# Filler matmuls placed by TensorE's row activity, and other durations in a scheduling list

## The chip, the core and the metric

The kernel runs on one NeuronCore of a Trainium2 chip. The metric is the device time of one execution in microseconds (us), the median of three runs. One more execution was recorded by the hardware profiler; all durations below are from that one. The engines are TensorE (PE in the profile; PEld is its weight load), VectorE (DVE), ScalarE (ACT), GpSimd (POOL) and SyncE (SP), which here only issues DMAs.

## What is computed

Input x has shape (8, 256, 32, 32). Four layers follow each other, all in float32:

```python
# layer 0, per image: attention with 4 heads (q, k of 32 channels, v of 64), then a gated feed-forward
attn = softmax(einsum('bhkn,bhkm->bhnm', q, k) * SCALE)          # 1024 x 1024 for each head
out = einsum('bhdm,bhnm->bhdn', v, attn) + bn(dwconv3(v))
x = x + gamma1 * bn(conv1x1(out));  x = x + gamma2 * edffn(ln(x))
# layer 1: attention with 8 heads of 32 channels, then a small MLP
attn = softmax(einsum('bhdi,bhdj->bhij', q, k) * temp);  out = einsum('bhdj,bhij->bhdi', v, attn)
# layer 2: three quantized convolutions and a residual
# layer 3: a selective scan over 1024 positions, along rows and columns, forwards and backwards
dA = exp(dt[:, :, None] * A)                                      # A: 512 channels x 16 states
h = h * dA + dt[:, :, None] * B[:, None, :] * u[:, :, None]
y = einsum('bdn,bn->bd', h, C)
out = (y + x * D) * silu(z) @ W_out.T                             # the four directions are added
```

The first three layers work on one image at a time and are exact up to rounding; the fourth has 8 images x 4 directions.

## The kernel before, in words

**Two phases.** `phase_a` (from line 265) does layers 0 to 2 for the eight images and leaves layer 2's result in DRAM as bf16 codes. `phase_b` (from line 1142) does layer 3. Phase B starts when phase A has ended.

**The list.** Neither phase writes out its instruction order. Both are made of Python generators, called strands, that yield an operation (`_Op`), or a list of operations of one engine, or a condition to wait for. `_Order.run` (line 236) is a greedy list scheduler that runs while the program is built: for each ready strand it works out when its next operation could start (`start`, line 223), from when the engine becomes free, when the operands were written or last read, and 0.35 us between engines; it takes the earliest, then the strand's rank. `_Op.__init__` (line 103) gives each operation a planned duration, `cost`. The strand can override it: the maxima's matmuls yield 1.06, the scores' matmuls `SCORES`, and a list on TensorE gets `order.way` on top. `_Op.blocks` (line 129) cuts a tile into blocks of 512 elements; the list sees conflicts between operations by block. None of this exists on the chip: there, each engine runs its own instructions in the order that the list left, and waits at semaphores for real operands and buffers. So a planned duration changes only the order.

**Rooms.** `_Room` is a numbered set of equal buffers; `take` and `put` borrow and return one. In phase A the eight PSUM banks are one room (`bank`). In phase B the banks are four for `py`, three for `db` and one for `pp`.

**Phase A's two kinds of attention work.** `maxima` does a first pass for the softmax: two or four matmuls with 32 rows each (K = 32) fill two or four banks, then for each bank VectorE takes the maximum of each row (`tensor_reduce` into `stats`) and ScalarE the exponentials' sum (`activation` with `bias` and `accum_out`). `exponentials` then does the second pass: four score matmuls (K = 32), four that subtract the logarithm of the sum (`minus`, K = 3), four exponentials on ScalarE, four products with v. Strands of several images run side by side, held back by banks and ranks. Layer 0's feed-forward puts depthwise 3 x 3 taps on VectorE (`scalar_tensor_tensor`), ScalarE and GpSimd.

**Phase B's loop.** There are 64 blocks: 8 images x 2 orders of positions x 2 directions x 2 halves. Each block has 16 groups, one for each state. A group is four dbu = du x B on ScalarE (`scales`), 16 transposes into `db` (`turns`), four da = exp(dt x A) on ScalarE (`decays`, five buffers), four scans h on VectorE (`scans`), two products h x C on GpSimd (`products`) and 16 transposes into `py` that add up over the states (`sums`). Beside this, `ahead` starts the next blocks' work at fixed groups: the convolution `mixed` (xi with cvd into `pp`), the projection `dt` (xd with w_dt), and at group 6 `tables`: one list on ScalarE with a table load, Silu on xs, a table load, Softplus on dt, and the load of the exponential's table. The list marks dt as done at the end of that whole list. Then GpSimd forms tmp = dt x xs four times, TensorE transposes each into `pp`, and VectorE copies it to du, which the next block's dbu needs.

**Fillers.** `fill`, inside `phase_a` (line 1059), is called before each TensorE operation of phase A. If the planned gap, less 0.35 us, has room for at least one step of `FILL` = 0.3 us, it emits that many bf16 matmuls of `minus` (all -1) with itself, 128 rows x 512 columns, into a free bank, or into the operation's own bank. Their results are overwritten. The profile shows them as L1081. Phase B has none: its list has no `fill`.

## Time and profile before

| what | us |
|---|---|
| median of 3 runs (lowest to highest) | 10310.45 (10307.8 to 10314.3) |
| the profiled execution | 10303.42 |
| its span, first to last instruction | 10301.6 |
| busy in the span: PE, ACT, DVE, POOL | 9415.7, 8514.4, 7759.3, 6131.8 |

The profiled execution is 1.8 us longer than its span, and 7.0 us below the median. Phase A takes about the first 3690 us. `L136` in the profile is the line that emits every operation of the list, so groups are told apart by the names of their tiles. A float32 matmul of 512 columns stands in the trace as two MATMUL rows. "PEclk" is the share of TensorE's full clock that was granted. A busy engine in these views is one that has an instruction in flight; for TensorE that is not the same as an array in full use.

### The profile page before, as it was taken

The page shows a single profiled execution, that of the slowest core. Times are in us where ns is not written, and L with a number is a line of the kernel's source. Part 1 is how long each engine was busy: PE and PEld are TensorE (multiplying, and loading weights), DVE is VectorE, ACT ScalarE, POOL GpSimd, SP SyncE. Part 2 cuts the span into 40 slices and gives each one's busy share as a digit, 9 for nine tenths or more (in the row PEclk, how much of TensorE's full clock was granted, in tenths as well). Part 3 has the DMA queues.
Part 4 walks back from the last instruction along what each step waited for, and adds up shares of the span by engine and source line. Part 5 has one row for each costly group of instructions (what it writes and reads, how often), then busy time and mean ns, then how long its engine had stood idle before and what let it go on. Part 6 is the DMA issues. An engine that isn't in the chain of part 4 may idle for free.

```text
span 10301.6 us, 149772 instructions
## 1 busy us (share of the span) xinstructions
PE 9415.7 (91%) x55378; PEld 5953.1 (58%) x55499; DVE 7759.3 (75%) x8675; ACT 8514.4 (83%) x15869; POOL 6131.8 (60%) x2988
## 2 busy tenths in 40 slices
PE   9989989999999989989898999899989999989988
PEld 3333323333333347777776777777777777777676
DVE  6367467575667458888887888888888888888788
ACT  7867677867666759988898998989898889899888
POOL 1433032242121048878787787778787778787778
PEclk7988989989888899999999999999999999999999
DMA  2000000000000011112111112111111111111111
GB/s 58 30 19 17 21 21 19 17 26 17 13 17 9 17 34 51 53 44 59 46 52 53 46 52 59 43 52 56 49 51 48 56 50 49 55 52 46 57 43 52
DMA packets 219616, 415.83 MB, mean 40 GB/s; under 512 B 25137, under 2 KB 67505, under 8 KB 213762
## 3 DMA queue, kind: packets, MB, share of 16 engines
q1 hardware_dynamic: 218882, 406.24, 13.1%
q8 instruction: 437, 7.16, 0.3%
q14 instruction: 297, 2.43, 0.1%
HBM read 358.43 MB, written 37.22 MB: 38 GB/s over the span
## 4 chain that ended last, share of the span: by engine, by line
PE 28%; ACT 22%; DVE 8%; issue 3%; POOL 1%; DMA 1%; DVEq 0%; SPq 0%; POOLq 0%; ACTq 0%
PE pp L136 11%; PE py L136 9%; ACT da L136 9%; PE db L136 8%; ACT dbu L136 8%; DVE h L136 7%; ACT L136 2%; ACT xs L136 1%; ACT dt L136 1%; POOL h L136 1%; ACT L145 1%; DMA wi<-w_in 1%; DVE ys L136 1%; ACT st L136 0%; ACT z L136 0%
## 5 line engine op out<-in xcount | busy, mean ns | idle before, releaser
L136 POOL TENSOR_TENSOR h<-h,cb 128x1024 f32<-128x1024 f32 x2048 | 4813.3, 2373 | 1039.1 <-DVE h L136 367.0
L136 ACT ACTIVATE da<-dt,am 128x512 f32<-128x512 f32 x4096 | 2872.0, 714 | 543.2 <-DVE h L136 537.6
L136 ACT ACTIVATE dbu<-du,bT 128x512 f32<-128x512 f32 x4096 | 2798.1, 710 | 15.4 <-PE db L136 13.6
L136 PE MATMUL db<-ident,dbu 128*128 128x128 f32 x16384 | 2385.7, 280 | 362.2 <-DVE h L136 322.6
L136 DVE TENSOR_TENSOR_SCAN h<-da,db 128x512 f32<-128x512 f32 x2048 | 2338.9, 1202 | 460.2 <-ACT da L136 131.9
L136 DVE TENSOR_TENSOR_SCAN h<-da,st,db 128x512 f32<-128x512 f32 x2048 | 2465.9, 1262 | 258.8 <-ACT da L136 139.3
L136 PEld LDWEIGHTS db<-ident,dbu 128*128 128x128 f32 x16384 | 1885.2, 143 | 875.4 <-DVE h L136 539.6
L136 PE MATMUL py<-ident,h 128*128 128x128 f32 x16384 | 2141.8, 278 | 92.4 <-POOL h L136 75.5
L136 PEld LDWEIGHTS py<-ident,h 128*128 128x128 f32 x16384 | 1878.3, 143 | 227.0 <-POOL h L136 144.2
L136 DVE TENSOR_REDUCE stats<-bank 128x1 f32<-128x512 f32 x1536 | 983.4, 684 | 545.1 <-PE bank L136 544.0
L136 ACT ACTIVATE bank<-bank,stats 128x512 f32<-128x512 f32 x1536 | 1024.9, 672 | 432.1 <-DVE stats L136 424.5
L136 PE MATMUL bank<-big,big 32*128 32x512 f32 x4096 | 987.3, 713 | 37.9 <-ACT bank L136 27.7
L136 POOL TENSOR_TENSOR mid<-mid,mid 128x961 f32<-128x961 f32 (+2 forms) x192 | 397.2, 2076 | 992.9 <-ACT mid L136 663.6
L136 ACT ACTIVATE exps<-bank 128x512 f32<-128x512 f32 x1536 | 796.5, 620 | 165.9 <-PE bank L136 156.6
L136 PE MATMUL pp<-xi,cvd 128*128 128x512 f32 x1488 | 687.8, 598 | 1.6 <-DVE ys L136 1.6
L136 PEld LDWEIGHTS bank<-big,big 32*128 32x128 f32 x4096 | 334.7, 204 | 523.7 <-issue 219.7
L136 DVE SCALAR_TENSOR_TENSOR mid<-mid,cols,mid 128x961 f32<-128x961 f32 (+1 forms) x384 | 601.6, 1567 | 6.3
L136 PE MATMUL bank<-exps,big 128*32 128x512 f32 (+1 forms) x3072 | 547.9, 621 | 3.7 <-ACT exps L136 3.7
L136 PE MATMUL bank<-big 32*128 32x512 f32 x2048 | 517.4, 724 | 32.1 <-ACT bank L136 21.5
L136 POOL TENSOR_TENSOR tmp<-dt,xs 128x512 f32<-128x512 f32 x256 | 320.9, 1273 | 322.0 <-ACT dt L136 224.4
L136 POOL TENSOR_SCALAR big<-big,ga,gs 128x512 f32<-128x512 f32 x64 | 67.7, 1070 | 712.3 <-DVE gs L136 385.5
L136 POOL TENSOR_TENSOR big<-big,mid 128x961 f32<-128x961 f32 (+1 forms) x128 | 315.2, 2472 | 270.7 <-ACT mid L136 268.6
(204 smaller groups left out, 9116.4 us busy)
## 6 DMA issues: line engine op xcount, KB each, us to landing
cb<-c_d SPq DMA_DIRECT2D x1024, 256.0 KB, 3.3
wi<-w_in SPq DMA_DIRECT2D x192, 192.0 KB, 3.5
big<-in_x_dram SPq DMA_DIRECT2D x16, 1024.0 KB, 5.0
kept<-big SPq DMA_DIRECT2D x16, 1024.0 KB, 4.5
big<-kept SPq DMA_DIRECT2D x16, 1024.0 KB, 4.8
xf<-codes SPq DMA_DIRECT2D x48, 256.0 KB, 3.8
big<-big SPq DMA_DIRECT2D x16, 512.0 KB, 6.5
codes<-low SPq DMA_DIRECT2D x32, 256.0 KB, 2.0
```

Of the source, the lines that this page charges most:

```text
L136: return getattr(getattr(nc, self.engine), self.method)(*self.args, **self.kw)
L145: nc.scalar.preload_act_table_set("natural_log_exp_and_others")
```

## The change

It does four things.

- `fill` goes. `_Order.keep_dense` takes its place and is called for each TensorE operation in both phases. Each operation gets `rows`: its rows over 128, times its streaming time at full clock, half of that for transposes. The list keeps the planned activity of the last 3.4 us. Where that, with the operation itself, is under half of the window, or the planned gap is over 1.7 us, it emits fillers of 0.22 us into the buffer that came free first (or the operation's own fresh bank), as many as the gap holds, or up to 0.66 us past the time at which TensorE is free. Phase B gets a tile `minus` of its own and lends its `db` and `pp` banks.
- Planned durations change for all engines: among them, VectorE's three-operand operation between SBUF tiles of 961 elements from 1.07 to 1.45 us, ScalarE's maxima operation from 0.615 to 0.83 us, a decay or scale from 0.615 to 0.628 us; the maxima's matmuls from 1.06 to 0.9, `SCORES` from 1.3 to 1.12, `way` from 0.1 to 0.05.
- Blocks of small tiles become 64 elements instead of 512.
- A buffer that a DMA reads counts as read 2.1 us later.

```diff
@@ _Op.__init__
+        points = sum(math.prod(a.shape[1:]) == 1 for a in ins)
         if engine == "tensor":
...
+            self.rows = x.shape[0] / P * n * (0.44 if x.dtype != F32 else 1.72)
+            self.rows *= 0.5 if move else 1
         elif engine == "vector":
...
-            self.cost = 0.04 + n * (2.2 if scan else 0.57 if fast else 1.1) + (0.3 if fast or both else 0)
+            if method == "tensor_tensor_scan":
+                self.cost = 0.03 + 2.15 * n + 0.05 * points
+            elif both or three:
+                self.cost = 0.04 + 1.5 * n
+            elif fast:
+                self.cost = 0.04 + 0.9 * n
+            else:
+                self.cost = 0.05 + 1.09 * n + 0.05 * points
         elif engine == "scalar":
-            self.cost = 0.05 + 0.87 * n + (0.13 if len(ins) > 1 else 0)
+            self.cost = 0.05 + 0.06 * near + 0.85 * n + 0.093 * points + 0.17 * ("accum_out" in kw)
         elif engine == "gpsimd":
-            self.cost = 0.17 + 2.17 * n if method == "tensor_tensor" else 0.3 + n
+            self.cost = 0.12 + 2.2 * n if method == "tensor_tensor" else 0.07 + (2.0 if out.dtype == BF16 else 1.5) * n
@@ _Op.blocks
-        return [(a.name, k) for k in range(lo // 512, hi // 512 + 1)]
+        unit = 64 if step <= HALF else HALF
+        return [(a.name, k) for k in range(lo // unit, hi // unit + 1)]
@@ _Order
+    WINDOW, DENSE, DUMMY = 3.4, 0.5, 0.22
+
+    def keep_dense(self, t, cost, ops):
+        work = sum(o.rows for o in ops)
+        free, end = self.free.get("tensor", 0.0), t + cost
+        self.rows = [r for r in self.rows if r[1] > end - self.WINDOW]
+        seen = sum(w * (b - max(a, end - self.WINDOW)) / (b - a) for a, b, w in self.rows)
+        n = math.ceil((self.DENSE * self.WINDOW - seen - work * min(1.0, self.WINDOW / cost)) / self.DUMMY)
+        n = max(n, math.ceil((t - free - self.DENSE * self.WINDOW) / self.DUMMY))
+        if n > 0:
...
+            begin = max(free, since)
+            n = min(n, int((max(t, free + 0.66) - begin) / self.DUMMY))
+            if since < 1e9 and n > 0:
...
+                for _ in range(n):
+                    self.nc.tensor.matmul(x, lhsT=self.minus, rhs=rhs, start=True, stop=True)
...
+                t = max(t, begin + n * self.DUMMY)
+        self.rows.append((t, t + cost, work))
+        return t
@@ _Order.run
-            if self.fill and e == "tensor":
-                self.fill(t, ops)
+            if self.rooms and e == "tensor":
+                t = self.keep_dense(t, cost, ops)
             for o in ops:
                 o.emit(self.nc)
                 for k in o.reads:
-                    self.read.setdefault(k[0], {})[k] = (t + cost, e)
+                    self.read.setdefault(k[0], {})[k] = (t + cost + 0.7 * o.landing, e)
@@ phase_a
-    MAXIMA, SCORES = 2, 1.3
+    MAXIMA, SCORES = 2, 1.12
...
-                yield (1.06, ops)
+                yield (0.9, ops)
...
-    order.fill, order.way = fill, 0.1
+    order.rooms, order.minus, order.way = [bank], minus, 0.05
@@ phase_b
+    order.rooms = [ps_room, pp_room]
+    order.minus = wp.tile([P, P], BF16, name="minus", tag="minus")
+    nc.gpsimd.memset(order.minus, -1.0)
```

More of the change, by code (lines that the diff above doesn't have):

```diff
@@ L113, in __init__ @@
             n = math.prod(x.shape[1:]) / 1024
+            self.rows = x.shape[0] / P * n * (0.44 if x.dtype != F32 else 1.72)
             move = method == "transpose" or kw.get("is_transpose", False)
-            self.cost = max(0.06, (0.22 if x.shape[0] < 20 else 0) + n * (0.93 if move else 0.44 if x.dtype != F32 else 1.76 if n > 0.2 else 2.1))
+            self.cost = max(0.06, (0.22 if x.shape[0] < 20 else 0) + n * (0.96 if move else 0.44 if x.dtype != F32 else 1.76 if n > 0.2 else 2.0))
+            self.rows *= 0.5 if move else 1
         elif engine == "vector":
@@ L118, in __init__ @@
             both = near and method == "tensor_tensor"
-            scan = method == "tensor_tensor_scan"
-            self.cost = 0.04 + n * (2.2 if scan else 0.57 if fast else 1.1) + (0.3 if fast or both else 0)
+            three = near and method == "scalar_tensor_tensor"
+            if method == "tensor_tensor_scan":
[6 more added lines that the diff above has]
+                self.cost = 0.05 + 1.09 * n + 0.05 * points
         elif engine == "scalar":
-            self.cost = 0.05 + 0.87 * n + (0.13 if len(ins) > 1 else 0)
+            self.cost = 0.05 + 0.06 * near + 0.85 * n + 0.093 * points + 0.17 * ("accum_out" in kw)
         elif engine == "gpsimd":
-            self.cost = 0.17 + 2.17 * n if method == "tensor_tensor" else 0.3 + n
+            self.cost = 0.12 + 2.2 * n if method == "tensor_tensor" else 0.07 + (2.0 if out.dtype == BF16 else 1.5) * n
         else:
@@ L183, in __init__ @@
         self.free, self.written, self.read, self.base, self.last = {}, {}, {}, {}, {}
-        self.fill, self.way = None, 0.0
+        self.rooms, self.minus, self.way, self.rows, self.fresh = [], None, 0.0, [], {}
     def add(self, rank, strand):
@@ L213, in takes @@
             self.base[t.name] = self.last.get((room.tag, k), 0.0)
+            if room in self.rooms:
+                self.fresh[t.name] = t
             out.append(t)
@@ L234, in start @@
         return t
+    WINDOW, DENSE, DUMMY = 3.4, 0.5, 0.22
[7 more added lines that the diff above has]
+        if n > 0:
+            since, room, k = min(
+                ((self.last.get((r.tag, k), 0.0), j, k) for j, r in enumerate(self.rooms) for k in r.left),
+                default=(1e9, 0, 0),
+            )
+            x = self.fresh.get(ops[0].args[0].name)
+            if x is not None and self.base[x.name] < since:
+                since, room = self.base[x.name], None
+            begin = max(free, since)
+            n = min(n, int((max(t, free + 0.66) - begin) / self.DUMMY))
+            if since < 1e9 and n > 0:
+                if room is not None:
+                    room = self.rooms[room]
+                    room.left.remove(k)
+                    room.left.insert(0, k)
+                    x = room.take()
+                rhs = self.minus.unsqueeze(1).to_broadcast([P, 4, P])
+                for _ in range(n):
+                    self.nc.tensor.matmul(x, lhsT=self.minus, rhs=rhs, start=True, stop=True)
+                if room is not None:
+                    room.put(x)
+                    self.last[room.tag, k] = begin + n * self.DUMMY + self.LATENCY
+                self.rows.append((begin, begin + n * self.DUMMY, n * self.DUMMY))
+                t = max(t, begin + n * self.DUMMY)
+        self.rows.append((t, t + cost, work))
+        return t
     def run(self):
@@ L256, in run @@
                 for k in o.reads:
-                    self.read.setdefault(k[0], {})[k] = (t + cost, e)
+                    self.read.setdefault(k[0], {})[k] = (t + cost + 0.7 * o.landing, e)
                 for k in o.writes:
+                    self.fresh.pop(k[0], None)
                     self.written.setdefault(k[0], {})[k] = (t + cost + o.landing, e)
@@ L286, in phase_a @@
     OTHERS = 3
-    MAXIMA, SCORES = 2, 1.3
+    MAXIMA, SCORES = 2, 1.12
     GATE = 1
-    FILL = 0.3
     big = _Room(rooms, "big", NBIG, [P, CC, N])
@@ L1057, in emit @@
             nc.scalar.preload_act_table_set("natural_log_exp_and_others")
-    def fill(gap, ops):
-        free, o = order.free.get("tensor", 0.0), ops[0]
-        spare = min(bank.left, key=lambda k: order.last.get((bank.tag, k), 0.0), default=None)
-        own = o.method == "matmul" and o.kw["start"] and o.args[0].shape[-1] == HALF and o.kw["rhs"].shape[0] > 3
-        since = min(
-            [order.last.get((bank.tag, k), 0.0) for k in bank.left] + [order.base.get(o.args[0].name, 0.0)] * own,
-            default=1e9,
-        )
-        n = int((gap - max(free, since) - 0.35) / FILL)
-        if n < 1:
-            return
-        if spare is not None and order.last.get((bank.tag, spare), 0.0) <= since:
-            bank.left.remove(spare)
-            bank.left.insert(0, spare)
-            t = bank.take()
-        else:
-            t = None
-        out = o.args[0] if t is None else t
-        rhs = minus.unsqueeze(1).to_broadcast([P, 4, P])
-        for _ in range(n):
-            nc.tensor.matmul(out, lhsT=minus[:, : out.shape[0]], rhs=rhs, start=True, stop=True)
-        if t is not None:
-            bank.put(t)
-    order.fill, order.way = fill, 0.1
+    order.rooms, order.minus, order.way = [bank], minus, 0.05
     stage = [0] * B
```

## The prediction

> **What bounds the kernel now.** I read the page's slices first, then the windows table by stage, then windows on stretches at low clock, last the order in time inside them. The page gives TensorE's busy tenths and its granted clock:

> ```profile
> PE   9989989999999989989898999899989999989988
> ...
> PEclk7988989989888899999999999999999999999999
> ```

> By stage (us, then busy us and count of PE, PEld, DVE, ACT, POOL, then clock, DMA share, GB/s), phase A and the body of phase B:

> ```profile
> 0.00:3690.00 3690.00, 3460.72 (x14923) 1280.33 (x14923) 2220.47 (x3297) 2630.62 (x5719) 907.14 (x470) 0.89 0.06 21
> ...
> 3900.00:10180.00 6280.00, 5683.53 (x38842) 4478.63 (x38959) 5316.94 (x5161) 5655.86 (x9767) 5012.54 (x2396) 0.97 0.17 51
> ```

> Phase A: TensorE has work 94% of the time, ScalarE 71%, and the clock is 0.89. The trace grants 1 or 0.5, so 22% of phase A, about 812 us, is at half clock. Phase B: ScalarE is nearest its limit (90%), the clock is 0.97. Here are phase A's longest stretches at half clock and two short ones:

> ```profile
> 101.50:193.70 92.20, 91.66 (x217) 39.81 (x217) 66.74 (x104) 82.14 (x215) 27.90 (x13) 0.50 0.01 3
> 989.00:1036.80 47.80, 47.80 (x116) 19.04 (x115) 42.20 (x68) 37.03 (x107) 3.54 (x3) 0.50 0.00 1
> 2931.00:2968.00 37.00, 36.64 (x83) 11.25 (x81) 27.94 (x46) 21.71 (x60) 0.00 (x0) 0.50 0.00 0
> 3207.00:3272.00 65.00, 65.00 (x153) 24.66 (x153) 52.64 (x85) 42.59 (x118) 2.06 (x1) 0.51 0.00 0
> 3504.00:3535.00 31.00, 30.65 (x73) 9.59 (x72) 22.81 (x41) 16.57 (x47) 0.00 (x0) 0.51 0.00 1
> 2630.00:2654.00 24.00, 23.93 (x52) 8.49 (x52) 20.05 (x35) 17.59 (x50) 0.00 (x0) 0.52 0.00 0
> 572.00:586.00 14.00, 10.62 (x20) 5.14 (x20) 4.95 (x8) 13.97 (x31) 5.02 (x3) 0.52 0.00 0
> 555.00:569.00 14.00, 8.74 (x12) 3.16 (x12) 13.89 (x14) 8.97 (x18) 8.53 (x4) 0.52 0.00 0
> ```

> In the six long ones TensorE has an instruction in flight all the time and is still at half clock: "busy" is not what the clock follows. They are the maxima, whose matmuls use 32 rows, two at a time. Single rows of the order in time (start, us, engine, ...) give the prices: two matmuls of the maxima at full clock (four rows of the trace) and nine at half, one and two fillers, two of ScalarE's maxima operations:

> ```profile
> 1503.89 0.39 PE L1081 MATMUL bank<-minus 128*128 128x512 bf16 x1
> 1507.37 0.60 PE L1081 MATMUL bank<-minus 128*128 128x512 bf16 x2
> 2063.31 1.13 PE L136 MATMUL bank<-big 32*128 32x512 f32 x4
> 3219.14 7.35 PE L136 MATMUL bank<-big,big 32*128 32x512 f32 x18
> 3224.08 0.66 ACT L136 ACTIVATE bank<-bank,stats 128x512 f32<-128x512 f32 x1
> 3224.74 0.66 ACT L136 ACTIVATE bank<-bank,stats 128x512 f32<-128x512 f32 x1
> ```

> So a filler costs TensorE 0.60 - 0.39 = 0.21 us. A pair of the maxima takes 1.13 less the tail that a lone filler shows beyond its step (0.39 - 0.21), some 0.9 us, at full clock, and 7.35 x 4 / 18 = 1.63 at half. ScalarE needs 2 x 0.66 = 1.32 for it. Phase B loses its clock where ScalarE loads tables for Silu and Softplus; two such places:

> ```profile
> 5838.00:5840.00 2.00, 1.14 (x11) 0.91 (x10) 0.00 (x0) 1.98 (x5) 1.56 (x2) 1.00 0.00 0
> 5840.00:5842.00 2.00, 0.42 (x4) 0.18 (x2) 0.00 (x0) 1.99 (x5) 2.00 (x2) 1.00 0.00 0
> 5844.00:5846.00 2.00, 1.33 (x7) 0.96 (x6) 2.00 (x3) 2.00 (x6) 0.48 (x1) 0.50 0.07 27
> ...
> 5648.00:5654.00 6.00, 5.21 (x19) 3.05 (x18) 3.55 (x3) 4.42 (x8) 6.00 (x3) 0.52 0.19 65
> 5654.00:5660.00 6.00, 5.83 (x31) 3.13 (x30) 1.37 (x2) 2.37 (x6) 6.00 (x4) 0.91 0.20 53
> ```

> TensorE starves at 5838 to 5842, the clock halves, yet ScalarE stays full: nothing is lost there. In the second place ScalarE idles 5.2 us (6 - 4.42 + 6 - 2.37) after the half clock.

> **The change part by part.**

> *Fillers in phase A.* By the order of instructions they go from 955 to 1749, and from 347 to 1032 between matmuls of the maxima; elsewhere they are few more. 794 x 0.21 = 167 us of TensorE. Among long runs of pairs there stand one to five, some 2.4 a pair: 0.9 + 2.4 x 0.21 = 1.4 us, against 1.63 at half clock and ScalarE's 1.32. Row activity is then (0.45 + 0.5) / 1.4 = 0.68, well over 0.45, so the clock holds.

> *What the clock gives in phase A.* In each long stretch the next engine bounds the gain: 92.2 - 82.14, 47.8 - 42.2, 37 - 27.94, 65 - 52.64, 31 - 22.81, 24 - 20.05 = 49 us of 297 together, 17%; the pair's 1.4 for 1.63 says 14%. In the other 515 us at half clock ScalarE or VectorE is often full, as in the two short rows, so I take half that rate, 8%: 41 us. Together 90; the neighbours won't run at 100%, so two thirds: 60 us saved. Bounds: 0 and 90.

> *Fillers in phase B.* 1056, or 222 us of TensorE, nearly all at groups 7 to 10 of a block, ahead of the transposes of tmp: 16 a block, 3.5 us, against 2 + 2 - 1.14 - 0.42 = 2.4 us idle at 5838 to 5842 and more up to 5844. The table list counts dt as done too late, so the first transpose of tmp, at 5839.77, will come some 2 us later; du is wanted only in the next block, which hides it. Without that cover it is 2 us x 62 = 124 us.

> *What the clock gives in phase B.* Only where ScalarE idles after the gap. That is in two of eight blocks: 5.2 us above with a further 1.3 at 5660 to 5666, and about 2 us near 5450; 8.5 x 8 images = 68 us. Fillers stand there too, 28 to 30 a block. I take half: 30 us. Bounds: 0 and 68.

> *Fillers that do lie on the path.* The 109 of phase A outside the maxima, 23 us; I take 15, and 10 for waits for banks in phase B: 25 us lost.

> *The new durations.* They only reorder. VectorE's taps were planned at 1.07 us and now 1.45, against 1.57 in the trace: nearer. ScalarE's maxima operation goes from 0.615 to 0.83, against 0.66 from start to start: further off. Decays and scales go from 0.615 to 0.628; phase B's order on VectorE and GpSimd hardly changes, ScalarE's two streams interleave differently. No row prices a reordering; its size is bounded by ScalarE's idle time in phase B, 620 us, and by phase A's. I bound it at 100 us either way, by the half clock's own total gain, and take 0: one of the two large corrections helps, the other hurts. The DMA reading rule, smaller blocks and phase B's memset of one tile (0.2 us) go with this: 0.

> *Sum.* -60 - 30 + 25 = -65 us. The profiled execution at 10303.4 becomes 10238; the median stands 7.0 higher, so 10245.

> **Rivals.**

> 1. *The order gains too.* The taps' 384 operations no longer hold up the maxima behind them on VectorE. For it: ScalarE waits 424 us for `stats`. Against: the worse maxima duration. With 90 + 68 from the clock, no fill loss and some 30 from the order: 10310 - 188 = 10122.
> 2. *The clock is full and nothing follows.* The neighbours were the bound: gains 25, losses 25. For it: the short rows and 5844. Time 10310.
> 3. *Slower: the fillers make TensorE the bound of the maxima.* About two thirds of 768 pairs, 510, run at full clock now with 0.9 us under ScalarE's 1.32. The list plans ScalarE at 0.83, so 1.66 a pair, and fills for a gap that is 0.34 us narrower on the chip. A run of three to five makes the pair 1.5 to 1.95 us. At +0.3 us a pair, 153 us: 10245 + 153 = 10398. It decides from 65 / 510 = 0.13 us a pair. Against: the average of 2.4 gives 1.4, just at the point.
> 4. *It doesn't do what it says:* a stretch falls to half clock anyway, and its pair with fillers takes 1.63 + 2.4 x 0.43 = 2.7 us. Its row activity is then about 0.7, too little to return at once. 100 pairs would cost 107 us: 10350.

> **How the numbers follow.** Forecast 45%, rival 1 12%, rival 2 8%, rival 3 25%, rival 4 10%. A measurement here tells apart about 0.2%, 21 us. Faster 0.57, same 0.08, slower 0.35. Predicted 10245; its own range, from the bounds 0 to 90, 0 to 68 and the losses, is 10150 to 10290. The order's 100 us and rivals 1 and 3 widen it to 10080 to 10420.

> **What would show it.** Right: phase A's clock at 0.96 or more, no half-clock stretch over 15 us in the maxima, ScalarE busier in them; phase B at 0.99, with ScalarE's idle time after the gaps of two blocks in eight gone. Fillers hidden: no row of the waits in which ScalarE waits longer for `stats` than 424 us. Wrong: phase A is longer at a full clock (rival 3), the clock stays near 0.89 (rival 4), or phase B changes by more than 70 us, which would be the order's work.

## The result, and the profile after

| | before | after |
|---|---|---|
| median, us (lowest to highest, 4 runs each) | 10312.38 (10307.8 to 10321.5) | 10261.17 (10247.5 to 10281.83) |
| ratio, 95% interval | | 0.9952 [0.9939, 0.9964] |
| profiled execution, span | 10303.42, 10301.6 | 10256.65, 10254.8 |

The change saves 51 us, 0.5%; the forecast was 65. The sum came and its parts did not. The page's slices after:

```profile
PE   9999999999999989999999999999999999999998
...
PEclk9998999999999999999999999999999999999999
```

The windows by stage (us, then busy us and count of PE, PEld, DVE, ACT, POOL, then clock, DMA share, GB/s):

```profile
0.00:3690.00 3690.00, 3492.14 (x15717) 1243.67 (x15717) 2202.61 (x3291) 2635.16 (x5723) 921.63 (x474) 0.94 0.07 21
3900.00:10180.00 6280.00, 5832.44 (x40216) 4512.66 (x40214) 5357.52 (x5197) 5697.23 (x9827) 5051.02 (x2412) 1.00 0.18 52
```

Phase A's clock went from 0.89 to 0.94, yet ScalarE is busy only 4.5 us more in the same window (2635.16 for 2630.62). Phase B is at 1.00. Where the phases part is read from the tile view of `db`: its first transpose is the start of phase B's loop (count, then ns min/median/max, then first and last start).

```profile
L147 PE MATMUL db<-ident,dbu x16384: 270/273/477, 3769.7 to 10220.1; 128*128 128x128 f32 x200
```

The same row before:

```profile
L136 PE MATMUL db<-ident,dbu x16384: 272/273/477, 3763.5 to 10264.1; 128*128 128x128 f32 x200
```

So up to here the kernel is 6.2 us *later*, and the rest takes 6485.1 us (10254.8 - 3769.7) for 6538.1 (10301.6 - 3763.5): 53.0 us less. The costliest groups (busy us, mean ns | idle before, what ended it), four of before and then five of after:

```profile
L136 PE MATMUL db<-ident,dbu 128*128 128x128 f32 x16384 | 2385.7, 280 | 362.2 <-DVE h L136 322.6
L136 DVE TENSOR_REDUCE stats<-bank 128x1 f32<-128x512 f32 x1536 | 983.4, 684 | 545.1 <-PE bank L136 544.0
L136 ACT ACTIVATE bank<-bank,stats 128x512 f32<-128x512 f32 x1536 | 1024.9, 672 | 432.1 <-DVE stats L136 424.5
L136 PE MATMUL bank<-big,big 32*128 32x512 f32 x4096 | 987.3, 713 | 37.9 <-ACT bank L136 27.7
```

```profile
L147 ACT ACTIVATE da<-dt,am 128x512 f32<-128x512 f32 x4096 | 2863.9, 714 | 506.0 <-DVE h L147 502.0
L147 PE MATMUL db<-ident,dbu 128*128 128x128 f32 x16384 | 2329.7, 276 | 194.7 <-DVE h L147 157.7
...
L147 DVE TENSOR_REDUCE stats<-bank 128x1 f32<-128x512 f32 x1536 | 987.9, 684 | 655.0 <-PE bank L147 652.2
L147 ACT ACTIVATE bank<-bank,stats 128x512 f32<-128x512 f32 x1536 | 1024.7, 672 | 409.2 <-DVE stats L147 395.3
L147 PE MATMUL bank<-big,big 32*128 32x512 f32 x4096 | 928.3, 667 | 15.7 <-ACT bank L147 9.0
```

The maxima's matmuls are shorter (667 ns for 713), but VectorE waits longer for the banks they fill (652.2 us for 544.0): what their higher clock gave was lost again on TensorE. The page doesn't say to what; the experiments below do. In phase B the transposes' idle time fell from 362.2 to 194.7 us.

### The profile page after: what moved, and what is told of

Same layout as the page of the kernel before. It is cut to its first block, busy times and chain, and to the rows that moved or that the text cites. A ratio compares the mean times of both kernels' runs of the same rounds, so it can differ in the third digit from the quotient of the medians.

```text
span 10254.8 us, 153646 instructions
## 1 busy us (share of the span) xinstructions
PE 9573.8 (93%) x57349; PEld 5920.9 (58%) x57349; DVE 7741.9 (75%) x8671; ACT 8521.2 (83%) x15873; POOL 6150.3 (60%) x2993
## 4 chain that ended last, share of the span: by engine, by line
ACT 28%; PE 22%; DVE 10%; issue 2%; POOL 1%; DMA 1%; DVEq 0%; SPq 0%; POOLq 0%; ACTq 0%
ACT da L147 11%; ACT dbu L147 10%; PE pp L147 9%; DVE h L147 8%; PE py L147 7%; PE db L147 6%; ACT L147 2%; ACT xs L147 1%; ACT dt L147 1%; DMA wi<-w_in 1%; POOL h L147 1%; ACT L156 1%; DVE ys L147 1%; ACT st L147 1%; ACT z L147 0%
## 5 line engine op out<-in xcount | busy, mean ns | idle before, releaser
L147 ACT ACTIVATE da<-dt,am 128x512 f32<-128x512 f32 x4096 | 2863.9, 714 | 506.0 <-DVE h L147 502.0
L147 PE MATMUL db<-ident,dbu 128*128 128x128 f32 x16384 | 2329.7, 276 | 194.7 <-DVE h L147 157.7
L147 PEld LDWEIGHTS db<-ident,dbu 128*128 128x128 f32 x16384 | 1855.6, 141 | 798.8 <-DVE h L147 350.4
L147 PE MATMUL py<-ident,h 128*128 128x128 f32 x16384 | 2099.2, 274 | 95.4 <-POOL h L147 90.0
L147 PEld LDWEIGHTS py<-ident,h 128*128 128x128 f32 x16384 | 1837.4, 141 | 236.4 <-POOL h L147 179.2
L147 DVE TENSOR_REDUCE stats<-bank 128x1 f32<-128x512 f32 x1536 | 987.9, 684 | 655.0 <-PE bank L147 652.2
L147 ACT ACTIVATE bank<-bank,stats 128x512 f32<-128x512 f32 x1536 | 1024.7, 672 | 409.2 <-DVE stats L147 395.3
L147 PE MATMUL bank<-big,big 32*128 32x512 f32 x4096 | 928.3, 667 | 15.7 <-ACT bank L147 9.0
L277 PEld LDWEIGHTS <-minus 128*128 128x128 bf16 x2805 | 260.6, 101 | 663.4 <-issue 463.8
L277 PE MATMUL bank<-minus 128*128 128x512 bf16 x1749 | 508.5, 414 | 52.5 <-ACT bank L147 41.1
L147 PEld LDWEIGHTS bank<-big,big 32*128 32x128 f32 x4096 | 283.2, 191 | 463.0 <-issue 267.4
L147 POOL TENSOR_TENSOR big<-big,mid 128x992 f32<-128x992 f32 (+1 forms) x128 | 324.4, 2542 | 290.1 <-ACT mid L147 287.4
```

What stands on the lines that cost most here:

```text
L147: return getattr(getattr(nc, self.engine), self.method)(*self.args, **self.kw)
L277: self.nc.tensor.matmul(x, lhsT=self.minus, rhs=rhs, start=True, stop=True)
```

## The experiments

The question was why the clock pays in phase B and not in phase A. Three theories stood at the start. **O**: the new order loses what the clock gives. **N**: the neighbours (ScalarE, VectorE) were the bound of phase A, so the clock is worth nothing there. **F**: the fillers lie on TensorE's path and eat the gain. The table has every run; "to db" is where the first transpose into `db` begins, "rest" the span less that, "half" the time at half clock in either part, all from the profiled execution, "sent" the fillers of either phase. Each ratio is against executions of before taken together with that run; their medians lie between 10307.3 and 10312.4.

| run | sent A / B | half A / B | to db | rest | median, us | ratio to before, 95% |
|---|---|---|---|---|---|---|
| before | 955 / 0 | 850 / 387 | 3763.5 | 6538.1 | 10312.38 | |
| after | 1749 / 1056 | 437 / 41 | 3769.7 | 6485.1 | 10261.17 | 0.9952 [0.9939, 0.9964] |
| x1 | 1391 / 0 | 887 / 488 | 3869.3 | 6550.4 | 10420.64 | 1.0104 [1.0089, 1.0119] |
| x2 | 1250 / 899 | 625 / 219 | 3791.1 | 6549.3 | 10343.75 | 1.0024 [1.0010, 1.0037] |
| x3 | 0 / 0 | 1236 / 454 | 3804.7 | 6547.8 | 10350.09 | 1.0034 [1.0021, 1.0047] |
| x4 | 1343 / 1001 | 440 / 89 | 3670.6 | 6502.7 | 10191.27 | 0.9880 [0.9865, 0.9895] |
| y1 | 0 / 1056 | 1225 / 68 | 3775.1 | 6489.2 | 10262.41 | 0.9951 [0.9934, 0.9967] |
| y2 | 727 / 1056 | 884 / 55 | 3794.8 | 6488.6 | 10299.30 | 0.9991 [0.9984, 0.9998] |
| y3 | 1343 / 1056 | 447 / 55 | 3683.1 | 6491.8 | 10172.29 | 0.9862 [0.9847, 0.9876] |
| y4 | 1203 / 1056 | 597 / 48 | 3737.2 | 6488.3 | 10213.99 | 0.9906 [0.9891, 0.9921] |
| z1 | 1749 / 0 | 492 / 410 | 3783.1 | 6536.0 | 10313.09 | 1.0004 [0.9995, 1.0013] |
| z2 | 0 / 1056 | 1085 / 55 | 3729.5 | 6489.1 | 10214.20 | 0.9906 [0.9892, 0.9921] |
| z3 | 1343 / 1056 | 567 / 67 | 3778.9 | 6488.9 | 10272.15 | 0.9968 [0.9957, 0.9979] |
| z4 | 1748 / 1056 | 358 / 61 | 3685.6 | 6486.9 | 10164.30 | 0.9861 [0.9844, 0.9877] |

### One part of the change alone (x1, x2)

x1 is the kernel before with the new durations, blocks and read times and the old `fill`; x2 is the kernel after with the old durations, blocks and read times. Of x1's edit:

```diff
-            self.cost = 0.05 + 0.87 * n + (0.13 if len(ins) > 1 else 0)
+            self.cost = 0.05 + 0.06 * near + 0.85 * n + 0.093 * points + 0.17 * ("accum_out" in kw)
...
-    MAXIMA, SCORES = 2, 1.3
+    MAXIMA, SCORES = 2, 1.12
```

> The new durations, blocks and read times with the fillers of before: the old rule in phase A, none in phase B. Phase A is read up to the first transpose into db (before 3763.5 us, after 3769.7), phase B from there to the end (6538 and 6485). Phase A: if the new order loses what the clock gives (theory O), it is about 3800 us; if the neighbours are the bound (N) or the fillers lie on the path (F), about 3765. Phase B: if the fillers' clock is the gain, 6538; if the new durations are, 6485.

> The new fillers in both phases with the durations of before. Phase A: O says about 3725 us, N and F say about 3765. Phase B: 6485 if the clock is the gain, 6538 if the durations are. Clock 0.94 or more in phase A.

Both are slower than before, and the change that has both is faster: the parts don't add up. No theory had foreseen this: up to `db` it is 3869 us in x1, where 3800 was the highest figure expected, and 3791 in x2, where 3765 was; x2's rest is 6549 and not 6485 or 6538. Much of phase A's loss comes early. The 192nd of ScalarE's maxima operations, the last one before a long pause, ends at 335.5 us in x1 and 324.5 in x2, for 273.7 before: 62 of the 106 us that x1 loses up to `db`, and 51, more than the 28 that x2 loses there. Windows there, x1 first, then x2:

```profile
150.00:200.00 50.00, 50.00 (x102) 11.96 (x101) 22.74 (x36) 29.73 (x75) 11.33 (x5) 0.50 0.00 0
```

```profile
150.00:200.00 50.00, 50.00 (x102) 11.31 (x101) 22.10 (x35) 26.32 (x73) 2.64 (x2) 0.50 0.00 0
```

ScalarE is busy only 29.73 and 26.32 of 50 us, at half clock, with fillers among the matmuls.

### No fillers, and fewer (x3, x4)

x3 takes the fillers out of the kernel after, so that its list doesn't plan them either; x4 lowers the target and counts transposes whole.

```diff
-    order.rooms, order.minus, order.way = [bank], minus, 0.05
+    order.way = 0.05
-    order.rooms = [ps_room, pp_room]
```

> The changed kernel without any filler. Phase A's clock falls to 0.85 or less. N says that phase A stays within 20 us of 3770; if the clock is worth what the forecast says (14 to 17% of the long stretches), it is 3830 or more. Phase B: 6538 if the clock is the gain there, 6485 if the durations are.

```diff
-    WINDOW, DENSE, DUMMY = 3.4, 0.5, 0.22
+    WINDOW, DENSE, DUMMY = 3.4, 0.4, 0.22
...
-            self.rows *= 0.5 if move else 1
```

> The changed kernel with a target of 0.4 instead of 0.5 and transposes counted fully: 1343 fillers in phase A instead of 1749, 1001 in phase B instead of 1056. F says that phase A falls by 20 us or more, to 3750 or less, at nearly the same clock; N says 3765 to 3775. Phase B stays at 6485.

x3's 3804.7 lies between the two figures that its theories set, 3790 and 3830. The same 50 us in x3 and in after:

```profile
150.00:200.00 50.00, 49.17 (x131) 31.26 (x132) 40.62 (x77) 46.19 (x134) 6.48 (x3) 0.50 0.00 1
```

```profile
150.00:200.00 50.00, 50.00 (x191) 13.96 (x191) 37.33 (x64) 43.78 (x122) 7.57 (x4) 1.00 0.00 1
```

This is the pair of lines to remember. At half clock *without* fillers ScalarE does as much (46.19) as at full clock with them (43.78), and far more than at half clock with them (29.73, 26.32 above). x4 is 99 us shorter up to `db` than after at nearly the same time at half clock, as F had it; its rest missed the expected 6485 by 18 us. But x3 and x4 also have other orders of the real work than after, since the list plans around the fillers; they cannot tell F from O. The next runs hold the order still.

### The order held, the fillers not sent (y1, y2, z1)

The list plans its fillers as in after, so that every real instruction keeps its place, but phase A's are not sent (y1), or n // 2 of each group are (y2); in z1 phase A's are sent and phase B's are not. y1:

```diff
+                m = 0 if len(self.rooms) == 1 else n
                 if room is not None:
...
-                for _ in range(n):
+                for _ in range(m):
```

> The kernel after with its order of all real instructions in the first phase kept as it is (the planner still counts its 1749 fillers there), but none of those fillers is sent to TensorE; the second phase and its 1056 fillers are as after. Theory F (fillers lie on the path of the first phase: 1749 x 0.21 us = 373 us of TensorE time at full clock, part of it in front of real matmuls): without them the clock falls, but the path is relieved; the first phase is about 3770 again within 40 us, the clock of it about 0.85, median 10230 to 10300. Theory C (the clock is what these fillers buy, and they stand in gaps as planned): as the clock falls to half for about 1200 us, the first phase loses a fourth of that and more, 4000 or more, median over 10450. Theory T (only the long stretches at half clock with fillers in between cost much): the first maxima end at about 192 us as in the run without fillers.

> As the kernel after with its order kept, but of each group of n fillers in the first phase only n // 2 are sent (727 of 1749). F: fewer fillers on the path at a clock that still mostly holds: the first phase ends 40 to 100 us earlier than the 3770 of after, median 10160 to 10220. C: the clock falls and the time grows, 3830 or more, median over 10320. O (the gain of the run with a target of 0.4 came from another order of the real work, not from fewer fillers): with the order unchanged and the clock mostly held, 3770 within 20, median 10245 to 10280.

> The kernel after with its order of all real instructions kept in both phases; its 1749 fillers of the first phase are sent, of the 1056 of the second none (the planner still counts them). Theory C (the gain of the second phase is the clock that they hold): without them the second phase has 300 us and more at half clock again and takes 6530 to 6555, median 10300 to 10325. Theory O (the gain is the order that the planner makes when it has the new durations and fillers): 6485 within 15 although the clock falls, median 10250 to 10275. Theory P (both, the order with a clock that only TensorE's stretches need): between, 6500 to 6530.

First the 50 us of above once more, in y1, which has the order of after:

```profile
150.00:200.00 50.00, 49.17 (x130) 31.33 (x132) 40.54 (x77) 46.20 (x134) 6.40 (x3) 0.50 0.01 2
```

So the pair of lines does not come from another order. y1: 1749 fillers fewer, 788 us more at half clock, and the same time (10262.41 and 10261.17). In phase A the fillers are worth nothing in sum, as theory F of y1 had it, and not C, which asked for 4000 us up to `db`. T came too: y1's 192nd maxima operation ends at 278.6 us, as x3's does. What the clock gives and what the fillers cost is taken apart below. z1: without the 1056 of phase B, its rest takes 6536.0, and that of before is 6538.1: the gain of phase B is the clock that they hold (theory C), the order adds 2 us. (The eight runs with the second phase of after take 6485.1 to 6491.8 for it, so the gain is some 44 to 51 us.) z1's waits of the transposes and decays, as the page has them:

```profile
L147 ACT ACTIVATE da<-dt,am 128x512 f32<-128x512 f32 x4096 | 2867.8, 714 | 524.9 <-DVE h L147 519.6
L147 PE MATMUL db<-ident,dbu 128*128 128x128 f32 x16384 | 2399.6, 282 | 309.2 <-DVE h L147 282.0
```

After has 506.0 and 194.7 in these places. With equal orders one can follow the delay from instruction to instruction: both traces have 15643 ScalarE rows with the same names in the same order. Counted from 3800 us on, z1 falls behind after through all of phase B, by 9.4 us at 5000, 17.3 at 6000, 24.8 at 7000, 34.1 at 8000, 40.0 at 9000 and 50.8 at the end. But not every block adds to it. Phase B repeats every eight blocks, and cut at each block's first transpose into `db` the delay adds up over the eight repetitions to this:

```
block of eight       1     2     3     4     5     6     7     8
delay, us in sum   14.4   0.6   4.5  15.0  -0.1  -0.9  -0.1  17.7
```

So it stands in four blocks of eight, some 2 us each time in blocks 1, 4 and 8 and 0.6 in block 3. Half clock is not confined to these: of the 387 us at half clock in phase B of before (z1 has 410), 27.3, 54.6, 23.9 and 54.6 us lie in blocks 2, 5, 6 and 7, in each of which z1's delay is 0.6 us or less over the eight repetitions.

The same measure explains phase A. Here is how far y1 is behind after (negative: ahead), over after's stretches at half clock of more than 8 us:

```
stretch of after at half clock      fillers in it   y1 behind after, us
 957 to 1009                         41               10.4 -> -8.8
1282 to 1306                         18                2.2 -> -6.6
1719 to 1736                          7               -6.6 -> -15.1
2538 to 2551, 2620 to 2637           33               -0.2 -> -5.1, -0.9 -> -7.0
all 19 stretches, 300 us            184              -54.7 in sum
outside them                                         +60.1 in sum
```

Outside these stretches the fillers gain 60 us. In 300 us in which the clock falls all the same, they lose 55, of which the five shown make 47. y1 is at half clock for most of these five too (69 to 100% of each), so it is hardly the clock that sets the two apart there. A fallen stretch need not cost anything: that of 517 to 531 holds 17 fillers and loses nothing. VectorE is busy for 13.93 of its 14 us in after and in y1 alike, and TensorE has time to spare (9.85 us busy in y1). So N does not hold for phase A as a whole: the clock is worth something there, and what it gives is lost again elsewhere. The windows around the worst one, after and then y1, both at nearly the same low clock:

```profile
949.00:1009.00 60.00, 58.71 (x137) 14.36 (x141) 41.60 (x66) 32.76 (x92) 2.51 (x2) 0.57 0.00 0
```

```profile
949.00:1009.00 60.00, 58.69 (x134) 29.22 (x132) 57.44 (x92) 44.05 (x126) 5.48 (x4) 0.56 0.00 0
```

And TensorE's order in time there, in after (start us, us, ...):

```profile
959.44 1.03 PE L277 MATMUL bank<-minus 128*128 128x512 bf16 x2
960.40 2.08 PE L147 MATMUL bank<-big,big 32*128 32x512 f32 x4
962.41 1.03 PE L277 MATMUL bank<-minus 128*128 128x512 bf16 x2
963.37 2.08 PE L147 MATMUL bank<-big,big 32*128 32x512 f32 x4
...
968.36 1.46 PE L277 MATMUL bank<-minus 128*128 128x512 bf16 x3
```

A pair of the maxima with its fillers takes 962.41 - 959.44 = 2.97 us, where ScalarE needs 1.32. At full clock a filler costs TensorE 0.22 us (0.82 us for three at 150.92 less 0.60 for two at 168.84), and outside the fallen stretches the fillers gain more than they cost, the 60 us above. At half clock each costs double (1.46 us for three less 1.03 for two, 0.43), and the two fillers in 2.97 us don't bring the clock back. The prediction's count of row activity, made for this trace, shows how the stretch differs from others. The window of 3.41 us ahead of the fall has 0.36. In the stretch all windows but the last have 0.48 to 0.68, the last 0.98. At full clock such windows nearly always kept it: of 2761 full-clock windows over 0.45 in this trace 4 are followed by half clock. At half clock they did not regain it: of 81 half-clock windows under 0.75 none is followed by full clock, and all 59 over it are. The target of 0.5 lies between the two figures. A trap: the fillers that should hold the clock make the low clock dear. In y2 the half portion misses the target more often: 80 us are lost in 38 such stretches, 61 gained outside, and it is the slowest of the four portions of this order (3794.8, which none of its three theories had).

Whether a stretch falls also differs from execution to execution. z1's phase A is the program of after, but its profiled execution fell to half clock at 565 to 609 and the other did not: 18 us, of which it is still 13 behind at the end of the phase. By the same count the window ahead of z1's fall had 0.28, while after's windows from 561 to 589 hold 0.42 or more. Twelve executions of z1 on one chip lie between 10298.3 and 10322.4, so a single execution's figure up to `db` is good to some 20 us. z1, then after:

```profile
560.00:610.00 50.00, 48.74 (x100) 12.66 (x99) 19.43 (x31) 33.16 (x75) 16.32 (x9) 0.56 0.00 0
```

```profile
560.00:610.00 50.00, 46.12 (x176) 15.54 (x175) 37.06 (x58) 44.30 (x110) 16.95 (x9) 1.00 0.00 1
```

### Fewer fillers or another order? (y3, y4, z2, z3, z4)

y3 has x4's rule in phase A and after's in phase B. y4 is y3 with one planned duration nearer to the trace. z2 has y3's order with none of its phase A fillers sent. z3 has after's order with 1343 sent, y3's number; z4 has y3's order with 1748, after's number.

```diff
+        if len(self.rooms) == 1:
+            self.DENSE = 0.4
+        else:
+            self.DENSE = 0.5
```

> The rule of the run with fewer fillers (target 0.4, transposes counted whole) in the first phase, the rule of after (0.5, transposes by half) in the second: fillers 1343 and 1056. If the two phases add up as their parts did (3671 of the fewer-fillers run, 6485 of after): span 10156, median 10165 to 10180. If the second phase of the run with fewer fillers (6503) is a matter of where the first phase leaves the queues, and not of its own fillers: 10190, as that run.

```diff
-            self.cost = 0.05 + 0.06 * near + 0.85 * n + 0.093 * points + 0.17 * ("accum_out" in kw)
+            self.cost = 0.05 + 0.06 * near + 0.85 * n + 0.093 * points + 0.0 * ("accum_out" in kw)
```

> The kernel y3 with one duration changed: ScalarE's pass over a maxima tile (with accum_out) costs 0.66 us in the list, as the trace has it from start to start, in place of 0.83; fillers 1203 and 1056. If the list's durations matter as such (a list that is nearer to the trace plans better): the first phase 20 to 60 us shorter than that of y3, median 10110 to 10150. If durations as such are worth nothing, within 15 us of y3. If the longer figure was what left room between the maxima pairs for other work: 20 us or more slower than y3.

> The kernel y3 (target 0.4 in the first phase, where it ended 3683) with its order of all real instructions kept, but none of its 1343 first-phase fillers sent; the second phase as in y3. Theory O (its first phase is 87 us shorter than that of after through the order that its planner happened to make): 3683 within 20, median 10160 to 10190, at a clock of about 0.93. Theory F (fewer fillers on the path at a clock that is still held): the clock is not held now, so it goes back to 3740 to 3790, median 10230 to 10290.

```diff
+                if len(self.rooms) == 1:
+                    self.due += n * self.SHARE
+                    m = int(self.due) - self.sent
+                    self.sent += m
```

`SHARE` is 0.768 in z3 and 1.302 in z4.

> The kernel after with its order of all real instructions; of its 1749 first-phase fillers 1343 are sent (each group shortened in proportion), as many as the kernel y3 sends. So far: 0 sent 3775, 727 sent 3795, 1749 sent 3770 (3783 in the run whose first phase was the same). Theory F (surplus fillers lie on the path and eat what the clock gives): the clock still mostly holds and 406 x 0.21 us = 85 us of fillers go, about half of them on the path: 3720 to 3745, median 10195 to 10230. Theory O (in this order the first phase is bound by neighbours, whatever TensorE does): 3765 to 3790, median 10250 to 10285. Theory H (a target that is missed by little drops the clock and then the fillers run at half clock): 3790 or more, median over 10280.

> The kernel y3 with its order of all real instructions; 1748 first-phase fillers are sent in place of 1343 (each group lengthened in proportion), as many as after sends. So far in this order: 0 sent 3730, 1343 sent 3683. Theory F: 405 more fillers of 0.21 us = 85 us, about half of them on the path, 3715 to 3740, median 10205 to 10235. Theory O (surplus fillers stand in gaps of TensorE that nobody waits for): 3683 within 15, median 10160 to 10190.

y3 comes out as the sum of its two phases (10165 to 10180 expected). F falls, as far as it puts the price at 30 us and more: z4's 405 added fillers, 85 us of TensorE, cost 2.5 us in the profile and nothing in the median (10164.30 for 10172.29), and z3 gains nothing by leaving 406 out. Both came as O had it. Surplus fillers are free in sum, not each by itself, for they also leave z4 89 us less at half clock. By the count above, 1343 fillers gain 91 us outside the fallen stretches and 1748 gain 76; in the order of after it is 71 with 1343, and 60 and 64 with 1749 (after and z1). That would be some 10 to 15 us for 85 us of fillers, from one execution each, and about as much less is lost inside the stretches. What sets y3 apart from after (86.6 us up to `db`) has two halves. The tile view of `db`, for y1, z2 and y3:

```profile
L147 PE MATMUL db<-ident,dbu x16384: 270/273/477, 3775.1 to 10229.7; 128*128 128x128 f32 x200
```

```profile
L147 PE MATMUL db<-ident,dbu x16384: 270/273/477, 3729.5 to 10183.9; 128*128 128x128 f32 x200
```

```profile
L147 PE MATMUL db<-ident,dbu x16384: 270/273/477, 3683.1 to 10140.1; 128*128 128x128 f32 x200
```

y1 and z2 both send nothing in phase A and differ in order alone: 45.6 us. z2 and y3 have one order: the fillers give 46.4. By the medians it is 48 and 42. z2's two theories, all order or all fillers, had neither foreseen this half and half. By the same count as above y3's fillers gain 91 us outside 22 half-clock stretches and lose 44 inside; y3's longest such stretch is 24 us, after's 51, z3's two of 48. So in y3 the trap is shallower. Durations nearer to the trace don't make a better list by themselves: y4, with one such duration, is 42 us slower than y3 in the median, the last of its three cases. It also sends 140 fillers less and is 150 us longer at half clock in phase A, so this is not shown to be its order alone. z2's gain over y1 was not traced to a place in the list; that stays open. So does x2's phase B: 899 fillers planned by the old durations leave 219 us at half clock and bring no time; no run held its order.

z4 is the best version, at 0.9861 [0.9844, 0.9877] of before, some 97 us under after by the medians.

## Why the prediction was right in sum and wrong in its parts

- **Bound, row activity.** Right. The clock rises with the rows that the fillers add: with them phase B rises to 1.00, phase A to 0.94; without (x3) it is 0.918 over the span for 0.977.
- **"What the clock gives in phase A", -60.** This is the step that failed, and the forecast named what it lacked. The gain is there: 60 us outside the long half-clock stretches. But the step took the clock as held ("row activity is then 0.68 ... so the clock holds"). It held in most stretches and not in 300 us of them, and in these the fillers cost 55. That is rival 4's mechanism: its pair was put at 2.7 us and takes 2.97; its price was 107 us, of which half came. The 0.68 that was to hold the clock did not regain it in a fallen stretch (0 of 81 windows under 0.75). It should have been a term of the sum, with a share of stretches that fall, and not a rival at 10%.
- **"What the clock gives in phase B", -30.** Right in kind, mis-sized: 51 us (z1 against after: 6536.0 - 6485.1), nearer to the bound of 68. The places were half right. The gain is in four blocks of eight, and the forecast looked at two of these: it put 2 us and 6.5 us on the first and the third, which give 1.8 and 0.6 each time. The fourth and the eighth, which give 1.9 and 2.2, it left out.
- **"Fillers that do lie on the path", +25.** About 0 in sum (z4); at full clock perhaps 10 to 15 us for 405 more. The +10 for phase B, for waits for banks, was the author's estimate; no run shows it alone, and it is inside the net 51.
- **"The new durations", 0.** The order without the fillers: phase A 3775.1 (y1) for 3763.5, which still held the old 955 fillers; phase B 6536.0 (z1) for 6538.1. 12 and -2, so 0 was a fair value, and the bound of 100 was needed: another target's order is worth 46 us (y1 against z2), x1's durations with the old fillers cost 108 by the medians.
- **Rival 3**, TensorE as the bound at full clock, did not come: more fillers in z4 cost nothing in sum.

So the sum: phase A -60 + 15 was forecast and +6 came (+12 order and old fillers, -60 and +55 new fillers); phase B -30 + 10 was forecast and -53 came (-51 fillers, -2 order). Two errors of about 51 and 33 us cancelled to 18: that the sum was near is luck.

Of the signs that the forecast named, two point at the step that failed: phase A's clock is 0.94 and not 0.96, and a stretch of 51 us in the maxima is at half clock, where none was to be over 15. Two others came: phase B is at 1.00, and ScalarE waits 395.3 us for `stats`, under the 424 named.

## What to carry to other kernels

In this kernel, work that only keeps the clock up was free or nearly so while the clock was up (an estimated 10 to 15 us for 405 fillers, 85 us of TensorE, by the count above), and cost double (0.43 us a filler for 0.22) where it had fallen and TensorE was the engine the others waited for. Ask first what happens in the stretches where it falls all the same, and count them apart. A target that holds a state need not be enough to regain it: here 14 windows of 0.48 to 0.68 in a row, all but one of them at the target of 0.5 or over, were each followed by half clock. To price an addition to a greedy list, keep its plan and leave the instruction out; without that, the new order (here some 46 us) hides the effect. With equal orders, the delay from instruction to instruction shows where each microsecond goes.

## What the hardware showed that was not expected

- In 50 us of the maxima ScalarE's busy time was 46.20 at half clock without fillers (y1), 43.78 at full clock with them (after, the same order), 29.73 at half clock with them (x1, another order).
- Half clock was regained only at a higher row activity than full clock needed to stay: in after, 4 of 2761 full-clock windows over 0.45 were followed by half clock, and 0 of 81 half-clock windows under 0.75 by full clock, but all 59 over 0.75.
- Two runs of one program differ by a stretch of 44 us at half clock that one has and the other has not, at a cost of 18 us (z1 and after, phase A).
